# Deformable convolution and mixture-of-experts convolution on one core: sampling in one run per band, one shared PSUM bank, and another order of table work

## The chip, the cores and the metric

The kernel runs on one core of a Trainium2 chip. Its engines work side by side: TensorE (PE; its weight loads are listed as PEld), VectorE (DVE), ScalarE (ACT), GpSimd (POOL) and SyncE (SP). Each takes its instructions in the order in which the program wrote them. SP, POOL and ACT also issue transfers (DMA). The metric is device time in microseconds, lower is better. Everything is in 32-bit floats.

## The reference

The input `x` has 8 images of 128 channels and 64 x 64 pixels. Two layers follow each other, each `x + layer(groupnorm(x))` with 32 groups.

```python
# layer 0: modulated deformable convolution, 3x3, then batch norm and relu
om   = conv3x3(x, off_w) + off_b                 # 27 maps: 9 y shifts, 9 x shifts, 9 masks
py   = row + ky - 1 + off_y;  px = col + kx - 1 + off_x
val  = bilinear(x, py, px) * sigmoid(mask)       # zero outside the image
out  = einsum('bckhw,ock->bohw', val, w) + b
out  = relu(batchnorm(out) * gamma + beta)
...
# layer 1: four expert convolutions 3x3, mixed per image by a gate, plus a shared one
scores  = sigmoid(mean(x) @ gate_w.T + gate_b)
weights = top2(scores) / sum
out = einsum('ebchw,be->bchw', conv3x3(x, expert_w), weights) + conv3x3(x, shared_w) + biases
```

A branch for shifts larger than the kernel's reach exists (`general`); with these inputs the shifts are small and it isn't taken.

## The kernel before

**Dense stage (layer 0).** `dense` treats the bilinear sampling as a matrix product. An image is cut into 8 bands of 8 rows; over 8 images there are 64 bands, numbered `g`. For each band:

- `pick(g)` (DVE, L635) copies pixel windows into `picked`; `pixels(g)` (L643) transposes them on PE in four runs of 4, 4, 4 and 3 (`pt`, L650), and ACT copies each run to `xt` (L655).
- `load_x(g)` (2 transfers, L619) and `load_y(g, k)` (8 transfers, L603) bring tent weights from tables in device memory into `xwts` and `ywts`; POOL issues them two bands ahead.
- `weights(n)` (DVE, L677) multiplies them to `s`, for one of five groups of a band; it is called three groups ahead.
- `sample(n)` multiplies `xt` with `s` on PE: 12 instructions into a pair of PSUM banks (`pq`, L693). ACT copies the pair into `samples` (L703). For the first and the last group DVE also copies one column out of `pq` (L715, L717).
- `close(g)` (L719) copies edge rows, among them four rows that the next band's tile needs.
- `conv(g)` runs nine taps (`py`, L745; two instructions a tap) over `samples`; ACT adds the bias into `y` (L753), DVE takes statistics (L754), SP stores `y` (L755). An image's last band has two such runs, of 5 and 4 rows.

The order within a band is written out by hand (`manual_schedule`): the groups of band `g` come in chunks of 2, 2 and 1, and after each chunk a third of the taps of band `g - 1`, with transposes of band `g + 1` between them.

**The tables** of image `b + 1` are made while image `b` is worked on, by the generator `tables(b)`: each `next` on it emits work up to its next `yield`, and `pause(n)` skips `n` such steps. It loads the image (SP, L260), takes group statistics (DVE, L272), a small product for the group mean and one for the variance (`pm`, `pv`), normalises in place (L300, L301), forms the shift and mask maps `om` with four products (`combine` on DVE, L327, and `tap` on PE, L344), writes them to device memory by rows and by columns (`rowwise`, `colwise`) and reads them back (`raw_off`), turns them into distances and masks, then into five tents on ACT (`tent`, L462, L464), and stores them: 28 transfers for x (`store_x`, L506, all on SP) and one for y (`store_y`, L487). The generator is emptied at the start of band 6 of an image, and the next one begins there with the image load.

For the first image the chain runs alone, ahead of the first band (the head): early tents for the first rows on ACT, their stores on POOL and SP, then the loads of bands 0 and 1.

PSUM has eight banks. Before: `ps_c` two banks (products of the chain), `ps_q` two pairs, `ps_y` one, `ps_t` one.

**Layer 1** loads `y` and `x`, normalises, and runs 3x3 products with transformed rows (`vs`, four groups, L1245 to L1249) on PE (L1329). `prepare(b)` makes weights and rows of an image; `prepare(0)` runs to its end before the first product is written.

Of the kernel before, what the change touches and what calls it, by code (L numbers as in the profile page):

```python
# [56 lines left out]
EARLY = 2  # L57
OFF_AT = 16
# [7 lines left out]
def deform_moe_conv(  # L66
# [112 lines left out]
    def dense():  # L179

        with ExitStack() as st:
# [5 lines left out]
            ps_c = st.enter_context(tc.tile_pool(name="ps_c", bufs=2, space=PSUM))  # L187
            ps_q = st.enter_context(tc.tile_pool(name="ps_q", bufs=2, space=PSUM))
            ps_y = st.enter_context(tc.tile_pool(name="ps_y", bufs=1, space=PSUM))
            ps_t = st.enter_context(tc.tile_pool(name="ps_t", bufs=1, space=PSUM))  # L190
# [55 lines left out]
            xts, ss = {}, {}  # L246
            bands = [(b, j) for b in range(B) for j in range(NB)]

            def tables(b):

                def pause(n):
                    for _ in range(n):
                        yield
# [4 lines left out]
                for q in range(4):  # L258
                    rows = slice(16 * q, 16 * q + 16)
                    nc.sync.dma_start(  # L260
                        out=pad[:, ROWPAD + 16 * q : ROWPAD + 16 * q + 16],
                        in_=x[b].rearrange("c (h w) -> c h w", w=W)[:, rows],
                    )
                    yield from pause(5)
                yield from pause(3)
# [10 lines left out]
                yield from pause(6)  # L276
                pm = ps_c.tile([P, CH], F32, name="pm", tag="pc")
                nc.tensor.matmul(pm[:, 0:1], lhsT=gsel, rhs=mv[:, 0:1], start=True, stop=True)
                yield from pause(4)
# [6 lines left out]
                yield from pause(3)  # L286
                pv = ps_c.tile([P, CH], F32, name="pv", tag="pc")
                nc.tensor.matmul(pv[:, 0:1], lhsT=gsel, rhs=ev, start=True, stop=True)
                yield from pause(4)
# [5 lines left out]
                yield from pause(4)  # L295
# [60 lines left out]

                for j in (1, 2):
                    yield from combine(j)
                yield from pause(2)
                tap(1, 1)  # L360
                tap(1, 0)
                yield from pause(6)
                tap(1, 2)
                tap(2, 1)
                yield from pause(3)
                nc.scalar.activation(even, taken(1), AF.Identity, bias=offb_sb)
                yield from combine(0)
                yield
                tap(2, 0)
                tap(2, 2)  # L370
                yield from pause(3)
# [3 lines left out]
                yield  # L375
                yield from combine(3)
                tap(0, 1)
                tap(0, 0)
                yield from pause(6)
                tap(0, 2)  # L380
                tap(3, 1)
                yield from pause(3)
                nc.vector.tensor_tensor(even, even, taken(0), ALU.add)
                yield from pause(3)
                tap(3, 0)
                tap(3, 2)
                yield from pause(4)
# [10 lines left out]
                for j in range(4):  # L398
# [4 lines left out]
                    nc.gpsimd.dma_start(  # L403
# [14 lines left out]
                for k in range(3):  # L418
# [6 lines left out]
                    for outs, parts, v in places:  # L425
                        nc.sync.dma_start(out=raw_off[parts, v], in_=by_row[outs, 0::2, k])
                        parts = slice(W + parts.start, W + parts.stop)
                        nc.gpsimd.dma_start(
# [6 lines left out]
                yield from pause(24)  # L435
# [14 lines left out]
                for i in range(2):  # L450
                    nc.vector.tensor_scalar(
                        raw_off[:, 2 * i, 0], raw_off[:, 2 * i, 0], nudge[:, i : i + 1],
                        None, ALU.add,
                    )
                nc.vector.tensor_copy(by_x, moved(1, 0, "j", "u", "v"))
# [10 lines left out]
                if b == 0:  # L466
                    n = 2 * EARLY * XSTEP
                    for i in range(NR):
                        for _ in tent(early_x[:, i], dist[W:P, 0:n], i, sides[1]):
                            pass  # L470
                nc.vector.tensor_copy(by_y, moved(0, 0, "v", "j", "u"))
                nc.vector.tensor_copy(by_y[:, :, 0, 0], raw_off[sides[0], :, 0, 2 * W])
                nc.vector.tensor_copy(by_y[:, :, W - 1, 2], raw_off[sides[0], :, 0, W - 1])
                yield from pause(2)
# [11 lines left out]
                def store_y():  # L486
# [3 lines left out]
                            offset=y_table[b].offset + (NR - 1) * YSTEP,  # L490
                            ap=[[GROW, H], [GROW - YSTEP, NR], [1, YSTEP]],
# [923 lines left out]
```

## Time and profile before

| | us |
|---|---|
| runs shown | 1569.37, 1573.36, 1578.78 (median 1573.36) |
| the profiled execution, device time | 1568.24 |
| its span | 1566.5 |
| head, to the first sampling product | 90.6 |
| dense stage, to the last tap | 1182.6 |
| layer 1, to the end | 1566.5 |

| engine | busy us | share of the span |
|---|---|---|
| PE | 1406.3 | 90% |
| PEld | 773.4 | 49% |
| DVE | 882.8 | 56% |
| ACT | 704.5 | 45% |
| POOL | 544.4 | 35% |

The span runs from the first to the last instruction. A line of a timeline gives start, length, engine, source line, operation, output and inputs with shapes, and a count where equal neighbours are merged; the bracket at its end is the idle time before it and what ended it. Lengths of matmuls overlap, since they are pipelined. "SPq" is a transfer issued by SP.

### The profile page before, as it was taken

The page shows a single profiled execution, that of the slowest core. Times are in us where ns is not written, and L with a number is a line of the kernel's source. Part 1 is how long each engine was busy: PE and PEld are TensorE (multiplying, and loading weights), DVE is VectorE, ACT ScalarE, POOL GpSimd, SP SyncE. Part 2 cuts the span into 40 slices and gives each one's busy share as a digit, 9 for nine tenths or more (in the row PEclk, how much of TensorE's full clock was granted, in tenths as well). Part 3 has the DMA queues.
Part 4 walks back from the last instruction along what each step waited for, and adds up shares of the span by engine and source line. Part 5 has one row for each costly group of instructions (what it writes and reads, how often), then busy time and mean ns, then how long its engine had stood idle before and what let it go on. Part 6 is the DMA issues. An engine that isn't in the chain of part 4 may idle for free.

```text
span 1566.5 us, 21056 instructions
## 1 busy us (share of the span) xinstructions
PE 1406.3 (90%) x7714; PEld 773.4 (49%) x7714; DVE 882.8 (56%) x1764; ACT 704.5 (45%) x1000; POOL 544.4 (35%) x856
## 2 busy tenths in 40 slices
PE   4069979998998999899999989999993799999998
PEld 1045545655555555555555555556552344444443
DVE  6345545546544654655455365533326888898872
ACT  2334634654464456447446644654543332333320
POOL 3543432533442343335335333533303222222200
PEclk9579989999999999999999999999996899999999
DMA  6366685887488657848856794777817144444111
GB/s 200 91 130 140 155 198 131 158 196 165 107 176 184 148 126 175 210 102 182 197 141 136 173 218 101 179 164 187 189 55 271 54 161 154 155 161 161 41 55 56
DMA packets 156414, 234.33 MB, mean 150 GB/s; under 512 B 104362, under 2 KB 110958, under 8 KB 147982
## 3 DMA queue, kind: packets, MB, share of 16 engines
q0 software_dynamic: 62304, 124.77, 36.3%
q1 hardware_dynamic: 93116, 107.91, 23.3%
q8 instruction: 62, 1.02, 0.3%
q14 instruction: 50, 0.41, 0.1%
q10 hardware_dynamic: 882, 0.22, 0.1%
HBM read 180.23 MB, written 52.32 MB: 148 GB/s over the span
## 4 chain that ended last, share of the span: by engine, by line
PE 72%; DMA 11%; ACT 4%; DVE 4%; SPq 2%; issue 2%; POOL 1%; DVEq 0%; POOLq 0%; ACTq 0%
PE py L745 27%; PE pc L1329 20%; PE pq L693 14%; PE pt L650 5%; PE pc L344 5%; DMA pad<-in_x_dram 3%; DMA xwts<-tabx 2%; DMA ywts<-taby 2%; DMA tabx<-work 2%; ACT samples L703 1%; SPq L506 1%; ACT pad L300 1%; ACT y L753 1%; DMA yd<-y 1%; DMA xt<-in_x_dram 1%
## 5 line engine op out<-in xcount | busy, mean ns | idle before, releaser
L745 PE MATMUL py<-samples,dw_sb 128*128 128x512 f32 (+3 forms) x1296 | 601.6, 575 | 17.3 <-ACT y L753 17.3
L603 POOL DMA_DIRECT2D ywts<-taby x504 | 294.2, 603 | 460.3 <-DVE s L677 270.7
L703 ACT COPY samples<-pq 128x864 f32<-128x864 f32 (+1 forms) x320 | 295.5, 963 | 193.0 <-PE pq L693 193.0
L693 PE MATMUL pq<-s,xt 64*128 64x144 f32 (+1 forms) x3840 | 314.0, 306 | 46.5 <-DVE s L677 45.0
L693 PEld LDWEIGHTS pq<-s,xt 64*128 64x128 f32 x3840 | 261.4, 190 | 151.9 <-issue 90.0
L745 PEld LDWEIGHTS py<-samples,dw_sb 128*128 128x128 f32 x1296 | 214.6, 190 | 170.5 <-issue 122.2
L677 DVE TENSOR_TENSOR s<-xwts,ywts 128x432 f32<-128x432 f32 (+1 forms) x448 | 208.4, 496 | 101.0 <-PE pq L693 90.2
L655 ACT COPY xt<-pt 128x512 f32<-128x512 f32 (+1 forms) x256 | 143.2, 559 | 229.5 <-PE pt L650 225.5
L650 PEld LDWEIGHTS pt<-ident,picked 128*128 128x128 f32 x960 | 121.1, 141 | 136.4 <-issue 120.1
L1329 PE MATMUL pc<-v,u 128*128 128x512 f32 x384 | 172.8, 599 | 9.3 <-DVE u L1278 9.3
L1329 PE MATMUL pc<-v,wmix 128*128 128x512 f32 x384 | 176.5, 605 | 0.0
L650 PE MATMUL pt<-ident,picked 128*128 128x128 f32 x960 | 148.7, 275 | 8.6 <-ACT xt L655 4.6
L754 DVE BATCH_NORM_STATS2 ystats<-y 128x6 f32<-128x512 f32 (+3 forms) x72 | 45.6, 633 | 144.5 <-ACT y L753 144.5
L717 DVE COPY samples<-pq 128x24 f32<-128x24 f32 x64 | 12.9, 202 | 192.4 <-ACT samples L703 192.4
L1329 PEld LDWEIGHTS pc<-v,u 128*128 128x128 f32 x384 | 72.4, 190 | 98.3 <-issue 85.6
L1329 PEld LDWEIGHTS pc<-v,wmix 128*128 128x128 f32 x384 | 72.6, 192 | 89.0 <-issue 85.3
L619 POOL DMA_DIRECT2D xwts<-tabx x132 | 75.9, 582 | 109.0 <-DMA tabx<-work 57.1
L1307 ACT ACTIVATE t<-pc,bmix 128x512 f32<-128x512 f32 x32 | 22.0, 687 | 183.2 <-PE pc L1329 101.2
L753 ACT ACTIVATE y<-py,db_sb 128x512 f32<-128x512 f32 (+3 forms) x72 | 45.9, 638 | 97.5 <-PE py L745 93.6
L635 DVE COPY picked<-pad 128x960 f32<-128x960 f32 x128 | 83.4, 693 | 0.0
L327 DVE TENSOR_TENSOR combo<-pad 128x1024 f32<-128x1024 f32 x64 | 75.2, 1217 | 9.9 <-PE pc L344 9.4
L1157 POOL TENSOR_TENSOR x<-x,xt 128x512 f32<-128x512 f32 x32 | 46.5, 1483 | 86.0 <-ACT x L1155 86.0
(154 smaller groups left out, 1024.3 us busy)
## 6 DMA issues: line engine op xcount, KB each, us to landing
xwts<-tabx POOLq DMA_DIRECT2D x126, 576.0 KB, 9.5
ywts<-taby POOLq DMA_DIRECT2D x504, 90.0 KB, 5.7
pad<-in_x_dram SPq DMA_DIRECT2D x48, 512.0 KB
out_dram<-yo SPq DMA_DIRECT2D x32, 512.0 KB
yd<-y SPq DMA_DIRECT2D x48, 256.0 KB
pad<-yd SPq DMA_DIRECT2D x16, 512.0 KB
x<-yd SPq DMA_DIRECT2D x16, 512.0 KB
xt<-in_x_dram SPq DMA_DIRECT2D x16, 512.0 KB
```

The lines of the kernel that those rows point to most:

```text
L327: nc.vector.tensor_tensor(combo_of[j][:, half * n : half * n + n], *rows, op)
L344: nc.tensor.matmul(pcs[j][32 * q : 32 * q + 32].rearrange("p (h w) -> p h w", w=W)[:, :, lo:hi], lhsT=weight_of[j][:, kx], rhs=combo_of[j] ...
L603: engine.dma_start(out=y_wts[g % 2][at : at + NR * Q, r].rearrange("p a b c -> p (a b c)"), in_=bass.AP(tensor=y_table[b].tensor, offset=y ...
L619: engine.dma_start(out=x_wts[g % 3][HALF * h : HALF * h + HALF, slot * XSTEP : (slot + n) * XSTEP], in_=bass.AP(tensor=x_table[b].tensor, ...
L635: nc.vector.tensor_copy(picked[g % 2][:, :, h], bass.AP(tensor=one.tensor, offset=one.offset, ap=[list(one.ap[0]), [T, NCOL], [W, Q], [1, Q]],
L650: nc.tensor.transpose(pt[:, c], picked[g % 2][:, c0 + c].rearrange("p h y x -> p (h y x)"), ident,)
L655: nc.scalar.copy(xts[g][:, c0 : c0 + n], pt[:, 0:n])
L677: nc.vector.tensor_tensor(s[:, :, 3 * at : 3 * (at + k)].rearrange("p m (c x) -> p m c x", x=3), by_x[:, :, c : c + k], by_y[:, :, w : w + ...
L693: nc.tensor.matmul(by_m[:, h, :, at : at + k], lhsT=xts[g][rows, c], rhs=s[rows, :, at : at + k], start=True, stop=True,)
L703: nc.scalar.copy(bass.AP(tensor=one.tensor, offset=one.offset + first, ap=[list(one.ap[0]), [M * PLANE, 2], [PLANE, M], [WB + 1, 3], [1, w ...
L745: nc.tensor.matmul(py, lhsT=dw_sb[:, 3 * (2 - yy) + 2 - xx], rhs=samples[g % 2][:, m : m + 3 * n - 2 : 3, xx, 1 : W + 1], start=(i == 0), ...
L1329: nc.tensor.matmul(pc, lhsT=us[j][:, kx], rhs=vs[g][:, rows, kx : kx + W], start=(kx == 0), stop=(kx == 2),)
```

## The change

- PSUM: `ps_c` has one bank instead of two, and the transposes `pt` use it too; `ps_q` has three pairs instead of two; `ps_t` is gone.
- In a band all five groups are sampled first, then come all taps, with transposes after taps 0, 1, 5 and 6. The chain's PE work is marked by a `yield BLOCK` and goes only after taps 3 and 8, one block at a time, a block being all three taps of one product. Transposes' second `yield` is gone.
- The two column copies out of PSUM per band become two copies inside `samples`, in `close`. `close` and the statistics of `y` are put off (`late`) until after the second group of the next band.
- The image load leaves `tables` for a generator of its own (`load_image`), which starts in the middle of band 5 instead of at band 6. Pauses in `tables` are changed, most of them shortened.
- Of the x stores of an image, two thirds are issued by SP and one third by POOL.
- For the first image: `colwise` stores are split between POOL and SP, reads of `colwise` between POOL and ACT; early tents are made by DVE (three operations each) instead of ACT; y distances come before x distances; `store_y` goes tent by tent; `load_y(0)` is issued by SP and ACT in turn; the second image's chain stops at its first block until band 0 is done.
- In layer 1 `prepare(0)` is left once its weights are ready, and the row transforms of groups 1 to 3 are emitted between the first products.

```diff
-            ps_c = st.enter_context(tc.tile_pool(name="ps_c", bufs=2, space=PSUM))
-            ps_q = st.enter_context(tc.tile_pool(name="ps_q", bufs=2, space=PSUM))
+            ps_c = st.enter_context(tc.tile_pool(name="ps_c", bufs=1, space=PSUM))
+            ps_q = st.enter_context(tc.tile_pool(name="ps_q", bufs=3, space=PSUM))
             ps_y = st.enter_context(tc.tile_pool(name="ps_y", bufs=1, space=PSUM))
-            ps_t = st.enter_context(tc.tile_pool(name="ps_t", bufs=1, space=PSUM))
...
+            def load_image(b):
+                if b >= B:
+                    return
+                for q in range(4):
+                    rows = slice(16 * q, 16 * q + 16)
+                    nc.sync.dma_start(
+                        out=pads[b % 2][:, ROWPAD + 16 * q : ROWPAD + 16 * q + 16],
+                        in_=x[b].rearrange("c (h w) -> c h w", w=W)[:, rows],
+                    )
+                    yield from pause(4)
...
+                def block(j):
+                    yield BLOCK
+                    for kx in (1, 0, 2):
+                        tap(j, kx)
+                    yield from pause(2)
...
-                        store_x(i, 0, (nc.sync,))
-                        yield from pause(4)
-                    store_y()
+                        store_x(i, 0, (nc.sync, nc.sync, nc.gpsimd))
+                        yield from pause(2)
+                    store_y(0, NR)
...
-                    pt = ps_t.tile([P, 4, P], F32, name="pt")
+                    pt = ps_c.tile([P, 4, P], F32, name="pt", tag="pc")
...
-                by_h = t[:, 6:30].rearrange("p (h m) x w -> p h m x w", h=2)
-                if q == 0:
-                    nc.vector.tensor_copy(by_h[:, :, :, 2, 1], by_m[..., 0])
-                if q == NGR - 1:
-                    nc.vector.tensor_copy(by_h[:, :, :, 0, W], by_m[..., wide - 1])
...
+                nc.vector.tensor_copy(t[:, 6:30, 2, 1], t[:, 6:30, 0, 0])
+                nc.vector.tensor_copy(t[:, 6:30, 0, W], t[:, 6:30, 2, W + 1])
...
-                    nc.vector.bn_stats(ystats[:, b, j + e, :], y)
+                    late.append((nc.vector.bn_stats, ystats[:, b, j + e, :], y))
...
-            CHUNKS = (2, 2, 1)
+                for q in range(NGR):
+                    if g < len(bands):
+                        weights(g * NGR + q + AHEAD)
+                        sample(g * NGR + q)
+                        if q == 0:
+                            load_x(g + 2, nc.gpsimd)
+                        if q in (2, 3):
+                            for k in range(T * (q - 2), T * (q - 1)):
+                                load_y(g + 2, k, nc.gpsimd)
+                    if q == 1:
+                        put_off()
+                taps = conv(g - 1) if g else iter(())
+                twice = 2 if g and bands[g - 1][1] == NB - 1 else 1
+                for done, _ in enumerate(taps):
+                    part, odd = divmod(done, twice)
+                    if odd == 0 and part in PIXELS:
+                        next(turned, None)
+                    if odd == 0 and part in BLOCKS and asked:
+                        asked = False
+                        tick()
+                    for _ in range(3 + (g < NB) if twice == 1 else 1 + done % 2):
+                        tick()
+                    if odd == 0 and part == 4:
+                        if g + 2 < len(bands):
+                            pick(g + 2)
+                        if j == NB - 3:
+                            loads = load_image(b + 2)
...
+                made[b] = vs, (wmix[:, 0], u1, u2, wmix[:, 2]), bmix
                 for g in range(NG):
                     if b or g:
                         transform(g, 1, nc.vector)
...
-            for _ in prepare(0, made):
-                pass
+            first = prepare(0, made)
+            while 0 not in made:
+                next(first)
```

`tick` advances the image load and, if no block is waiting, the chain; `put_off` runs what `late` holds.

## The prediction

> **What bounds the kernel now.** I read the busy shares first (TensorE, PE, 90%; VectorE, DVE, 56%; ScalarE, ACT, 45%), then PE's row in tables of stretches. The dense stage, from the first full band to the last, is this row (length, then busy time of PE, PEld, DVE, ACT, POOL, granted clock, DMA share, GB/s):
>
> ```profile
> 100.00:1182.00 1082.00, 1033.94 (x6712) 603.73 (x6711) 534.53 (x1129) 558.84 (x766) 410.43 (x689) 0.98 0.70 158
> ```
>
> PE is idle for only 48 of 1082 us, so the order of PE's own work is what counts, and a quiet band (no table work in it) shows what it costs. The timeline of PE, one full band (start, length, instruction, count; I use start to start, since lengths overlap):
>
> ```profile
> 1114.68 1.87 PE L693 MATMUL pq<-s,xt 64*128 64x216 f32 x24
> 1116.48 1.14 PE L745 MATMUL py<-samples,dw_sb 128*128 128x512 f32 x2
> 1117.46 0.60 PE L650 MATMUL pt<-ident,picked 128*128 128x128 f32 x4
> 1117.90 1.92 PE L745 MATMUL py<-samples,dw_sb 128*128 128x512 f32 x4
> 1119.65 0.60 PE L650 MATMUL pt<-ident,picked 128*128 128x128 f32 x4
> 1120.18 1.74 PE L693 MATMUL pq<-s,xt 64*128 64x144 f32 x24
> 1121.85 2.02 PE L745 MATMUL py<-samples,dw_sb 128*128 128x512 f32 x4
> 1123.71 0.60 PE L650 MATMUL pt<-ident,picked 128*128 128x128 f32 x4
> ...
> 1125.12 1.13 PE L693 MATMUL pq<-s,xt 64*128 64x144 f32 x12
> 1126.18 1.15 PE L745 MATMUL py<-samples,dw_sb 128*128 128x512 f32 x2
> ...
> 1129.34 0.89 PE L693 MATMUL pq<-s,xt 64*128 64x216 f32 x8
> ```
>
> The band takes 1129.34 - 1114.68 = 14.66 us with no wait. Sampling (pq) comes in three runs of two, two and one groups: 1.80, 1.67 and 1.06 us. Let a run cost a fixed f, a plain group m, a wider end group e: f+e+m = 1.80, f+2m = 1.67, f+e = 1.06, so m = 0.74, f = 0.19, e = 0.87. A tap of the convolution (two py instructions) between two pt takes (1119.65 - 1117.90)/2 = 0.875; next to a pq run it is 0.98, and two such taps 1.86 instead of 1.75. Four pt take 0.44 before py, 0.53 before pq. So each border of a pq run costs its neighbour 0.1 as well.
>
> Who waits for whom, from PE's table of waits (total, times, longest):
>
> ```profile
> PE pq L693 <- DVE s L677: 45.0, 5, 21.5
> PE pm L278 <- DVE mv L275: 38.2, 4, 24.6
> PE py L745 <- ACT y L753: 17.3, 15, 1.5
> ```
>
> The two longest belong to the head (before the first band). The other 23.5 and 13.6 us lie where one image ends and the next begins. There the timelines of SP, POOL and DVE read:
>
> ```profile
> 615.91 5.94 SPq L260 DMA_DIRECT2D pad<-in_x_dram  x4
> 616.12 1.11 POOL L619 DMA_DIRECT2D xwts<-tabx  x2 [10.76 <-DMA tabx<-work]
> 630.35 1.29 DVE L272 BATCH_NORM_STATS2 stats<-pad 128x6 f32<-128x512 f32 x2 [6.65 <-DMA pad<-in_x_dram]
> ```
>
> The image load starts only when the table stores in front of it on SP are out; POOL's table loads wait for the same stores; all then move at once (DMA share 1.04 from 620 to 640 us), and DVE, which runs in order, stands at the statistics while PE wants `s`.
>
> **The change, part by part.** Sums are against the profiled execution: span 1566.5, device time 1568.2 us. The three runs shown have median 1573.4, so I add 5.1 at the end.
>
> *Sampling in one run.* Two of three runs fall away in each of the 63 bands that have both sampling and taps: per run f = 0.19 plus two borders of 0.1, so 0.78 us a band, 49 us. That holds if the copies out of PSUM keep up:
>
> ```profile
> 1115.91 1.85 ACT L703 COPY samples<-pq 128x1008 f32<-128x1008 f32 x2 [0.38 <-PE pq L693]
> 1121.24 1.72 ACT L703 COPY samples<-pq 128x864 f32<-128x864 f32 x2 [0.36 <-PE pq L693]
> ```
>
> Clocking the new band from the start of its run: the groups end at 0.19+0.87 = 1.06, 1.80, 2.54, 3.28, 4.15. The first copy starts at 1.23 (1115.91 - 1114.68), the next 0.93, 0.80, 0.80, 0.80 later (a pair spans 1.85 or 1.72 where its last copy alone has 0.92): 1.23, 2.16, 2.96, 3.76, 4.56, ending at 2.26, 3.08, 3.88, 4.68, 5.59. With three pairs the fourth group needs the first copy (2.26, wanted 2.54), the fifth the second (3.08, wanted 3.28). Both fit, by 0.2 us. With two pairs the third group would wait for 2.26 instead of 1.80, and three hand-overs would give back nearly all of 0.78.
>
> The Trainium skill ("TensorEngine Tiling (Array Packing)", PSUM Bottleneck) speaks against this part: row tiling speeds up TensorE but not the emptying of PSUM, so the copy can become the limit. The row does show ACT (4.36 us for five) slower than PE (4.15); were the taps to wait for the last copy (5.59), the band would take 15.3 us and the part would lose 41 us instead of gaining 49; but the taps read the band before, so PE needs only the three pairs.
>
> *One PSUM bank for pt, pc, pm, pv.* A second pt run needs the copy of the first. Tap 0 ends at 5.13, pt 5.57, its copy runs 5.7 to 6.3 behind the last sample copy; tap 1 ends at 6.44. It fits by 0.1. The later pair (after taps 5 and 6) has the same spacing without copies ahead. Table products come in four runs of 24 in place of six of 16 (L344, 1.84 us for 16, 0.106 each at a steady pace, so about 0.15 a run and 0.2 of borders): two fewer for 7 images, 3 to 5 us, I take 3. In the head the four products lose their overlap with the readers of the bank: about 1.8 us.
>
> *Column fix and `close`.* 128 small DVE copies (L715 and L717, 0.20 us) out of PSUM become 128 inside SBUF. No row shows the new form; bounds 0.15 (the smallest DVE copies) and 0.28 (L725, 192 elements). Nothing on DVE here is on the path: what counts is that `close` now stands behind `s` of the fifth group (free to start at 1.2), bn_stats (0.69) and the fixes: 1.2+0.75+0.6+0.2+0.54 = 3.3 us into the band; the taps want it at 4.15. Cover 0.85 us. In bands with table work (combine, 1.2 us each, picked 1.28) DVE can come in 2 us late; then first the taps wait, then `s`.
>
> *Waits of py for y.* Of 17.3 us, about half are waits of 1.10 in bands where tents sit in front of y on ACT (seven); they are covered by the 4.15 us of sampling now: -8. The rest, between the two parts of an image's last band, stays. But the same tents now push the first sample copy: y at 1.95 in place of 0.8 moves PE's fourth group by 0.6. With the late `close`: +8 in all (bounds 0 and 40: no band, or 5 of 8 bands of 7 images by 1.1 us).
>
> *Image loads and table stores.* Loads are issued from the middle of the sixth band, some 10 us sooner; x stores go 2:1 to SP and POOL (SP L506 takes about 0.83 us per issue, 28 an image; POOL 0.6) and the pauses after the products shrink from about 96 to 75 steps, so the table is done more than a band before its load. What waits behind a POOL store for ACT's tent is the next table load, with some 4 us to spare. At stake: 37 us, and 9 for the slow matmuls after each stall (12 pq in 1.81 instead of 1.01 us at 496.9, clock 0.85). The bytes remain: the image's 2.1 MB and about 2.9 MB for the bands (1.2 MB of xwts and 0.7 of ywts a band, y out) in 18 us is above the 254 GB/s seen there, so I leave 2 to 3 us at each of six places: -30 (bounds -10 and -46).
>
> The skill ("DMA: Bandwidth & Descriptors", on issuing engines not being separate queues) says a second issuing engine saves only sequencer time. By that alone the two-queue part would be worth nothing once bytes bind, as the share of 1.04 says they do; the start 10 us earlier is what my number rests on.
>
> *Head.* First pq is at 90.59 because DVE stood for 19.4 us at shift L297 (POOL's pow behind table loads). That is now after the first band. But band 1 (103.07 now) needs `ywts` of its own, the last of POOL's loads (issued till 88.05, 5.7 to land). POOL's chain is 0.7 later by my count (products +1.8, split colwise and raw loads -1.9 and -0.8, by_y before by_x +1.1, early tents 15 DVE operations of about 0.25, bounds 0.15 and 0.41, for 10 on ACT of 3.4 in all): 94.5, then three `s`, picks, pm and pv, 4.5 us: 99. So -4 (bounds -10 and +2).
>
> *Layer 1 head.* DVE is busy without a gap from 1204 to 1236.9 and PE waits 9.5 us for its mv. The transforms are reordered, none removed: 0 (bounds -4 and +2).
>
> Sum: -49 -3 -8 +8 -30 -4 = -86: 1482 profiled, 1487 as a median.
>
> **The rivals.**
> (a) Copies or the shared bank set the pace: the 0.1 to 0.2 us of room is not there, and the 0.78 is given back. For: the room is small. Against: the clocking above. 1573 - 37 = 1536.
> (b) The change at the image border does not do what it says: bytes bind, and the stall only moves: -49-3-4-8+8+0 = -56: 1517.
> (c) Slower: `close` late on DVE. If DVE comes to it more than 0.85 us late, every tap row waits. It costs more than all gains together when PE waits 86/63 = 1.4 us in each band, that is DVE 2.2 us late in each. If all bands with table work (5 of 8, 39) waited 3 us: +117-86: 1604. For: DVE holds statistics and combines in order. Against: DVE is busy 534 of 1082 us, and quiet bands leave it idle for half their length.
>
> **How the numbers follow.** Forecast 0.64, (a) 0.16, (b) 0.13, (c) 0.07. The time is the forecast's 1487. Low end: border and head at their better bounds (-16 and -6), 1465; high end 1538, to take in (b) and (a). A difference under 0.5% (8 us) can't be told from none. Faster 0.91, same 0.02, slower 0.07.
>
> **What would show it.** After: a quiet band of 13.9 us with one pq run of 60 and about 4.2 us; hardly any wait of pq or pm for DVE in the dense stage; first pq near 76 and band 1 near 99 us; layer 1 as long as before. Wrong if pq waits for ACT's copies, pt for xt, or py for `close` in most bands.

## The result and the profile after

The changed kernel takes 1586.93 us (median of 7 runs, 1582.18 to 1589.91); the kernel before, run beside it on the same chip, takes 1577.12 us (7 runs). The ratio is 1.0064, 95% interval 1.0039 to 1.0089: 0.6% slower, where 5.5% faster was forecast. All ratios below are to the kernel before on the same chip. Line numbers differ from kernel to kernel (the sampling product is L693 before and L690 after); the tile names are the same. The profiled execution has device time 1584.7 and span 1582.8 us (before: 1568.2 and 1566.5).

The same row of the dense stage as before, from the first full band to the last (length, busy time of PE, PEld, DVE, ACT, POOL, granted clock, DMA share, GB/s):

```profile
100.00:1199.00 1099.00, 988.14 (x6652) 594.94 (x6648) 534.37 (x1128) 547.22 (x764) 441.92 (x743) 0.96 0.70 156
```

PE is idle for 111 us here; before it was 48. So PE's own work became shorter by 46 us (a few of these because 60 instructions had already run before 100 us), and its waits longer by 63. The timeline of PE in a quiet band shows the first half of this:

```profile
1119.01 4.25 PE L690 MATMUL pq<-s,xt 64*128 64x216 f32 x60
1123.19 1.15 PE L739 MATMUL py<-samples,dw_sb 128*128 128x512 f32 x2
1124.18 0.60 PE L648 MATMUL pt<-ident,picked 128*128 128x128 f32 x4
1124.62 1.04 PE L739 MATMUL py<-samples,dw_sb 128*128 128x512 f32 x2
...
1131.17 1.92 PE L739 MATMUL py<-samples,dw_sb 128*128 128x512 f32 x4
1133.02 4.25 PE L690 MATMUL pq<-s,xt 64*128 64x216 f32 x60
```

One run of 60 sampling instructions, no wait in it, and 14.01 us from run to run where it was 14.66. PE's table of waits over the whole execution shows the second half:

```profile
PE pq L690 <- DVE s L674: 84.7, 13, 25.5
PE pt L648 <- ACT xt L653: 30.8, 8, 17.4
PE pm L283 <- DVE mv L280: 23.0, 2, 12.4
...
PE pq L690 <- ACT samples L700: 11.0, 7, 1.7
```

The wait of 25.5 is the one before the first band. Of the other 59 us of `pq` for `s`, 53 lie at the borders of images 1 to 5 (in the kernel before, `pq` waited 45.0 for `s`, 21.5 of it before the first band); at the border of image 0 PE waits 12.4 us for `mv`. A border is the stretch around bands 6 and 7 of an image, where the image after next is loaded. One of these, in the timelines of PE, SP, POOL and DVE in turn:

```profile
622.16 4.21 PE L690 MATMUL pq<-s,xt 64*128 64x216 f32 x60
636.06 2.60 PE L690 MATMUL pq<-s,xt 64*128 64x216 f32 x36
651.77 3.49 PE L690 MATMUL pq<-s,xt 64*128 64x144 f32 x24 [13.10 <-DVE s L674]
```

```profile
625.38 1.02 SPq L259 DMA_DIRECT2D pad<-in_x_dram  x1
626.85 3.13 SPq L504 DMA_DIRECT2D tabx<-work  x4
630.36 0.63 SPq L485 DMA_DIRECT2D taby<-work  x1
631.04 2.59 SPq L259 DMA_DIRECT2D pad<-in_x_dram  x2
633.74 0.99 SPq L749 DMA_DIRECT2D yd<-y  x1
634.78 0.49 SPq L259 DMA_DIRECT2D pad<-in_x_dram  x1
```

```profile
632.07 1.15 POOL L617 DMA_DIRECT2D xwts<-tabx  x2 [7.33 <-DMA tabx<-work]
```

```profile
639.11 1.29 DVE L277 BATCH_NORM_STATS2 stats<-pad 128x6 f32<-128x512 f32 x2 [6.62 <-DMA pad<-in_x_dram]
645.86 1.29 DVE L277 BATCH_NORM_STATS2 stats<-pad 128x6 f32<-128x512 f32 x2 [5.46 <-DMA pad<-in_x_dram]
649.83 1.29 DVE L277 BATCH_NORM_STATS2 stats<-pad 128x6 f32<-128x512 f32 x2 [2.68 <-DMA pad<-in_x_dram]
651.03 1.25 DVE L674 TENSOR_TENSOR s<-xwts,ywts 128x432 f32<-128x432 f32 x3
```

The same border in the kernel before, PE and SP:

```profile
610.83 1.87 PE L693 MATMUL pq<-s,xt 64*128 64x216 f32 x24
635.33 1.81 PE L693 MATMUL pq<-s,xt 64*128 64x144 f32 x12 [3.35 <-DVE s L677]
```

```profile
614.55 0.65 SPq L487 DMA_DIRECT2D taby<-work  x1
```

Band 6 of image 3 starts at 622.16 (before: 610.83). The first image quarter is issued 3.2 us later, the other three 9 to 13 us later, behind x stores in SP's order; before, all four went out 5 to 11 us after that band's start. The y table's store stands 8.2 us behind the band's start; before it was 3.7. DVE takes all eight statistics ahead of the `s` that band 7 needs for its fourth group, and waits for each quarter; before, three stood ahead of the `s` that PE waited for, and the other five behind it.

How the time is spread over the images (to the last `y` of each, from the timeline of ACT, in us), with the forecast's terms added up per image (0.78 a band, 0.4 for products, 5 a border, 4 for the head):

| image | before | after | difference | forecast |
|---|---|---|---|---|
| 0, with the head | 252.5 | 268.9 | +16.4 | -15 |
| 1 | 134.0 | 129.3 | -4.7 | -12 |
| 2 to 5, mean of the four | 138.3 | 141.6 | +3.3 | -12 |
| 6, no new image to load | 129.7 | 127.3 | -2.4 | -7 |
| 7, no tables to make | 113.2 | 107.3 | -5.9 | -6 |
| layer 1 | 383.9 | 383.6 | -0.3 | 0 |

Image 7, with sampling and taps alone, is as forecast, in part by luck: 2.2 of its 5.9 us are one wait of PE in the kernel before (`pn` for `near`, 1085.25 in its trace) that the forecast didn't count. Image 6, which makes tables and loads no image, is off by 4 us, images 1 to 5, which do both, by 7 to 15. The table products don't fall into the same images in both kernels: images 0, 1 and 6 hold 240, 48 and 96 of their instructions (`pc`) where it was 224, 80 and 80, at 0.11 us each, so that 3.5 of image 1's 4.7 us only moved to other images.

### The profile page after: what moved, and what is told of

Same layout as the page of the kernel before. It is cut to its first block, busy times and chain, and to the rows that moved or that the text cites. A ratio compares the mean times of both kernels' runs of the same rounds, so it can differ in the third digit from the quotient of the medians.

```text
span 1582.8 us, 21300 instructions
## 1 busy us (share of the span) xinstructions
PE 1365.4 (86%) x7714; PEld 769.1 (49%) x7714; DVE 884.0 (56%) x1779; ACT 691.1 (44%) x990; POOL 573.6 (36%) x909
## 4 chain that ended last, share of the span: by engine, by line
PE 72%; DMA 12%; DVE 5%; ACT 4%; issue 3%; SPq 3%; POOL 1%; ACTq 0%; DVEq 0%; POOLq 0%
PE py L739 27%; PE pc L1345 20%; PE pq L690 13%; PE pt L648 6%; DMA pad<-in_x_dram 5%; PE pc L349 5%; DMA xwts<-tabx 3%; DMA tabx<-work 1%; SPq L504 1%; DMA ywts<-taby 1%; ACT samples L700 1%; ACT y L747 1%; DMA taby<-work 1%; DMA colwise<-om 1%; DVE combo L332 1%
## 5 line engine op out<-in xcount | busy, mean ns | idle before, releaser
L739 PE MATMUL py<-samples,dw_sb 128*128 128x512 f32 (+3 forms) x1296 | 573.6, 561 | 7.9 <-ACT y L747 6.1
L690 PE MATMUL pq<-s,xt 64*128 64x144 f32 (+1 forms) x3840 | 291.5, 306 | 95.7 <-DVE s L674 84.7
L700 ACT COPY samples<-pq 128x864 f32<-128x864 f32 (+1 forms) x320 | 282.6, 975 | 145.4 <-PE pq L690 145.4
L690 PEld LDWEIGHTS pq<-s,xt 64*128 64x128 f32 x3840 | 264.0, 194 | 141.5 <-issue 93.5
L674 DVE TENSOR_TENSOR s<-xwts,ywts 128x432 f32<-128x432 f32 (+1 forms) x448 | 198.5, 497 | 204.9 <-PE pq L690 116.6
L739 PEld LDWEIGHTS py<-samples,dw_sb 128*128 128x128 f32 x1296 | 219.1, 190 | 157.5 <-issue 126.8
L648 PEld LDWEIGHTS pt<-ident,picked 128*128 128x128 f32 x960 | 112.0, 142 | 175.4 <-ACT xt L653 108.0
L648 PE MATMUL pt<-ident,picked 128*128 128x128 f32 x960 | 153.3, 280 | 35.0 <-ACT xt L653 30.8
L617 POOL DMA_DIRECT2D xwts<-tabx x132 | 79.5, 613 | 65.9 <-DMA tabx<-work 41.5
L277 DVE BATCH_NORM_STATS2 stats<-pad 128x6 f32<-128x512 f32 x64 | 40.8, 683 | 88.3 <-DMA pad<-in_x_dram 88.3
L1172 POOL TENSOR_TENSOR pad<-pad,pad 128x512 f32<-128x512 f32 x28 | 39.5, 1442 | 71.7 <-ACT pad L1170 71.5
```

What stands on the lines that cost most here:

```text
L617: engine.dma_start(out=x_wts[g % 3][HALF * h : HALF * h + HALF, slot * XSTEP : (slot + n) * XSTEP], in_=bass.AP(tensor=x_table[b].tensor, ...
L648: nc.tensor.transpose(pt[:, c], picked[g % 2][:, c0 + c].rearrange("p h y x -> p (h y x)"), ident,)
L674: nc.vector.tensor_tensor(s[:, :, 3 * at : 3 * (at + k)].rearrange("p m (c x) -> p m c x", x=3), by_x[:, :, c : c + k], by_y[:, :, w : w + ...
L690: nc.tensor.matmul(by_m[:, h, :, at : at + k], lhsT=xts[g][rows, c], rhs=s[rows, :, at : at + k], start=True, stop=True,)
L700: nc.scalar.copy(bass.AP(tensor=one.tensor, offset=one.offset + first, ap=[list(one.ap[0]), [M * PLANE, 2], [PLANE, M], [WB + 1, 3], [1, w ...
L739: nc.tensor.matmul(py, lhsT=dw_sb[:, 3 * (2 - yy) + 2 - xx], rhs=samples[g % 2][:, m : m + 3 * n - 2 : 3, xx, 1 : W + 1], start=(i == 0), ...
```

## The experiments

**Is the gain of the run real, and what carries it?** Three kernels with two pairs of `pq`. The first (e1) is the kernel before with one edit:

```diff
-            CHUNKS = (2, 2, 1)
+            CHUNKS = (5,)
```

> The kernel before, with its five sample groups in one run and the taps behind them; two pairs of pq, the column fixes and the table chain stay as they were. Theory (the run itself is what gains, 0.65 us a band in quiet bands): with two pairs the third and later groups of a run wait some 0.1 us each for an ACT copy of 0.86 us against 0.84 us of products, so 0.3 to 0.65 us of 63 bands come back: -20 to -40 us, ratio 0.975 to 0.987. Rival (the third pair makes the gain): PE waits for ACT a full copy at each of three groups, 0.9 us or more a band against 0.65 saved: ratio 1.00 or above, and a wait of pq for samples above 50 us in all.

Measured: 1633.12 us, ratio 1.0374 (1.0330 to 1.0418). PE's waits in it:

```profile
PE pq L693 <- DVE samples L715: 51.7, 55, 2.0
PE pq L693 <- DVE s L677: 41.1, 6, 21.9
...
PE pq L693 <- ACT samples L703: 30.1, 51, 8.9
```

A quiet band takes 15.5 us. The theory missed: the run alone loses. The pair is held first by DVE's column copy out of PSUM, which waits for ACT's copy of the same samples, then by ACT's. The next kernel (e5) separates the two; it is the changed kernel with

```diff
-            ps_c = st.enter_context(tc.tile_pool(name="ps_c", bufs=1, space=PSUM))
-            ps_q = st.enter_context(tc.tile_pool(name="ps_q", bufs=3, space=PSUM))
+            ps_c = st.enter_context(tc.tile_pool(name="ps_c", bufs=2, space=PSUM))
+            ps_q = st.enter_context(tc.tile_pool(name="ps_q", bufs=2, space=PSUM))
```

> The changed kernel with two pairs for pq and two banks for the products and the transposes, in place of three and one; the run of five groups and the column fix in SBUF stay. e1_run_alone lost 0.85 us a band, and its waits name the column copies of each pair (samples, 51.7 us) before the ACT copies (30.1 us). Theory A (the column copies out of PSUM held the pairs): with the fix in SBUF two pairs cost only what ACT's copy is longer than the group and its notice, 0.1 to 0.5 us a band: +6 to +30 us against the changed kernel. Theory B (two pairs are too few in any case): as in e1, 1.0 to 1.5 us a band: +60 to +95 us. The second bank may give back 1 to 2 us at each image (waits of pc and pm for xt).

Measured: 1628.83 us, ratio 1.0342 (1.0313 to 1.0371), 44 us above the changed kernel: between the two theories. In a quiet band, which takes 15.2 us, the run of 60 is cut in three (timeline of PE):

```profile
1182.36 1.87 PE L690 MATMUL pq<-s,xt 64*128 64x216 f32 x24
1184.68 1.81 PE L690 MATMUL pq<-s,xt 64*128 64x144 f32 x24 [0.45 <-ACT samples L700]
1186.75 1.13 PE L690 MATMUL pq<-s,xt 64*128 64x144 f32 x12 [0.27 <-ACT samples L700]
1187.81 1.15 PE L739 MATMUL py<-samples,dw_sb 128*128 128x512 f32 x2
```

From 1182.36 to 1187.81 it is 5.45 us in place of 4.18. The two waits, 0.45 and 0.27, make 0.72 of the 1.27; the rest fits the run's fixed cost (0.19 by the forecast), paid again at each cut with some loss of overlap, which no run measured apart. So the third pair is what turns the run from a loss into a gain, and the column fix in SBUF is worth the 0.3 us a band between e1 and this.

The third (e11) puts the column fix into e1 (the copies out of PSUM go, two come into `close`), and so differs from e5 by the chain, the borders and the head:

```diff
-                if q == 0:
-                    nc.vector.tensor_copy(by_h[:, :, :, 2, 1], by_m[..., 0])
-                if q == NGR - 1:
-                    nc.vector.tensor_copy(by_h[:, :, :, 0, W], by_m[..., wide - 1])
...
+                nc.vector.tensor_copy(t[:, 6:30, 2, 1], t[:, 6:30, 0, 0])
+                nc.vector.tensor_copy(t[:, 6:30, 0, W], t[:, 6:30, 2, W + 1])
```

> The kernel before with the run of five groups and the column fix in SBUF, but two pairs, and its own table chain, image loads and head: against e5_two_pairs it differs by the chain, the borders and the head alone, against e1_run_alone by the column fix alone. Theory (chain, borders and head of the change cost some 25 to 40 us net where -37 was forecast): the quiet band is 15.1 us as in e5, and the time is that much below e5: ratio to before 1.008 to 1.02. Rival (chain and head cost nothing net, and the run's gain is smaller than the quiet bands say): as e5, 1.03 to 1.04.

Measured: 1626.05 us, ratio 1.0301 (1.0269 to 1.0333), quiet band 15.2 us. Against e5 the old chain and head save some 6 us only, hardly more than the noise, not 25 to 40. At the borders the old chain is no better here than the new one in e5: from the y of band 5 to the y of band 6 it takes, in images 0 to 5, 26.8, 23.6, 24.5, 25.6, 22.3 and 26.1 us, in all 148.9 (e5: 149.2), against 129.3 before and 165.5 in the changed kernel. Of the 20 us more than before the slower quiet band (0.5 us a band) explains 3.

It is tempting to put the other 17 to the single run itself. e1 stands against that: it has the same run and the same chain, and takes 131.4 us there in all. DVE's order doesn't explain it either: in e11, as before and in e1, three statistics stand ahead of the `s` that PE waits for. At the border of image 3 the first of them waits for its quarter until 666.54 in e11, 15.1 us after the quarter's issue, and until 664.03 in e1, 10.6 us after it. Why the quarter lands later in one of two kernels that differ in the column fix alone stays open.

**The head.** The changed kernel (e2) with image 1's chain driven two steps further before band 1:

```diff
-                    for _ in range(4):
+                    for _ in range(6):
                         next(made)
```

> The changed kernel with image 1's table chain driven two steps further before band 1, so that the pow of its scale stands on POOL ahead of the table loads of band 3. Theory (pow behind POOL's table loads holds shift, the normalisation on ACT behind it, the copies xt and so the transposes): the wait of 17.4 us of pt in band 1's taps goes to under 4, and the time falls by 12 to 17 us: ratio to before 0.995 to 0.999. Rival (band 1 to 3 wait for the x tables or the image's bytes in any case): the stall turns up at pq (for s, behind xwts) in band 2 or 3, and the time moves by less than 4 us.

First the changed kernel's own head, in the timelines of PE and POOL:

```profile
94.01 6.33 PE L690 MATMUL pq<-s,xt 64*128 64x216 f32 x58
...
124.89 0.90 PE L648 MATMUL pt<-ident,picked 128*128 128x128 f32 x3 [17.36 <-ACT xt L653]
```

```profile
109.22 1.13 POOL L617 DMA_DIRECT2D xwts<-tabx  x2
110.38 3.36 POOL L601 DMA_DIRECT2D ywts<-taby  x6
117.19 0.56 POOL L601 DMA_DIRECT2D ywts<-taby  x1 [3.44 <-DMA xwts<-tabx]
120.07 0.56 POOL L601 DMA_DIRECT2D ywts<-taby  x1 [2.32 <-DMA xwts<-tabx]
120.64 0.57 POOL L299 TENSOR_TENSOR scale<-ve,nhalf 128x1 f32<-128x1 f32 x1
```

Band 1 starts sampling at 94.01, earlier than the 103 us of before, and then its taps stop for 17.36 us. The 0.57 us of `pow` wait behind the table loads of two bands. `shift` on DVE waits for it, the normalisation on ACT for `shift` (17.56 us idle at L305), the copy `xt` stands behind that on ACT, and PE wants `xt`. In the edited kernel the same two lines are

```profile
106.91 0.57 POOL L299 TENSOR_TENSOR scale<-ve,nhalf 128x1 f32<-128x1 f32 x1
```

```profile
114.80 0.90 PE L648 MATMUL pt<-ident,picked 128*128 128x128 f32 x3 [6.89 <-ACT xt L653]
```

and image 0 ends at 260.8 in place of 268.9. Time: 1580.51 us, ratio 1.0042 (1.0015 to 1.0070). In the trace 8 us come back, half of what was expected: `shift` now stands on DVE behind four `s`, which wait 11.3 us for band 2's x table (to 109.46). The times alone can't tell this from the changed kernel.

**The borders.** The changed kernel (e3) with each quarter loaded when its rows are free (`load_image` here takes the quarters to load as a second argument):

```diff
-                        if j == NB - 3:
-                            loads = load_image(b + 2)
+                        freed = {0: 0, 2: 1, NB - 4: 2, NB - 3: 3}
+                        if g < len(bands) and j in freed:
+                            loads = load_image(b + 2, (freed[j],))
```

> The changed kernel with each quarter of the image after next loaded as soon as the last band that reads its rows has been picked (in bands 0, 2, 4 and 5) in place of all four in band 5 to 6. Theory (the stall of 12 to 13 us of pq at each image border comes from statistics waiting for quarters that land late, ahead of s in DVE's order): three of four quarters are there long before, only the last is waited for, and at each of six borders 7 to 11 us go: -40 to -65 us against the changed kernel, ratio to before 0.965 to 0.98. Rival (the border is bound by the bytes of the x table's stores and the table loads, the image counts little): the wait of statistics goes but s then waits for xwts as long; less than 15 us go, ratio 0.997 or above.

Measured: 1560.33 us, ratio 0.9907 (0.9876 to 0.9939). (Here the first quarter of image 2, one of 24, isn't loaded, since band 0 of image 0 has no taps in which the step falls.) 25 us less than the changed kernel, below the range expected. The wait tables from 270 to 1070 us say where the rest went. PE's waits for `s` fall from 58.6 to 5.6 us, but its waits for `y` rise from 4.1 to 17.8 and those for `mv` from nothing to 16.0. DVE, changed kernel:

```profile
DVE stats L277 <- DMA pad<-in_x_dram: 71.5, 18, 6.9
DVE shift L302 <- POOL scale L299: 14.7, 5, 4.5
DVE s L674 <- DMA xwts<-tabx: 1.5, 2, 0.8
```

and the kernel with spread quarters:

```profile
DVE s L674 <- DMA xwts<-tabx: 40.5, 7, 8.2
DVE shift L302 <- POOL scale L299: 32.7, 5, 8.6
```

The statistics wait no more, and two other waits take their place: `s` for the x table's loads, which wait for the x stores, and `shift` for a `pow` behind POOL's loads, as in the head.

Next, the gate of the chain's products (e4):

```diff
-            PIXELS, BLOCKS = (0, 1, 5, 6), (3, 8)
+            PIXELS, BLOCKS = (0, 1, 5, 6), range(9)
```

> The changed kernel with the 24 table products and the two small ones let in at any of the nine taps, not only at the fourth and ninth; the chain then ends some 40 steps (a band and a half) sooner. Theory (the gate makes the chain late: x stores end some 8 us after the border band's start, and the image's loads stand behind them on SP): the stores end before that band, the image's quarters are issued some 5 to 10 us sooner, and 4 to 8 us go at each of six borders: -25 to -45 us against the changed kernel, less 3 us for more changes of product shape. Rival (the quarter's landing is set by bytes, or statistics stand ahead of s in any case, and an earlier chain changes nothing): within 8 us of the changed kernel.

Measured: 1564.73 us, ratio 0.9932 (0.9903 to 0.9961): 21 us less than the changed kernel. At the border of image 3 the x stores now end 20 us before band 6 starts (596.9 against 617.4), and the statistics hardly wait for the image (2.3 us from 270 to 1070 us). PE waits 30.6 us for `s` there in place of 58.6. What holds DVE instead is the y table's loads:

```profile
DVE s L674 <- DMA ywts<-taby: 91.8, 11, 13.0
```

Is it the place behind the x stores on SP that makes the image late? The changed kernel with the quarters on ACT's queue (e10):

```diff
-                    nc.sync.dma_start(
+                    (nc.scalar if b > 1 else nc.sync).dma_start(
                         out=pads[b % 2][:, ROWPAD + 16 * q : ROWPAD + 16 * q + 16],
```

> The changed kernel with the image's four quarters issued on ACT's queue in place of SP's, at the same steps. Theory (the quarters are late because they stand behind the x stores on SP): they go out some 5 to 8 us sooner and PE's wait at a border falls by as much, -20 to -40 us against the changed kernel. Rival (the DMA engines are near 1.0 in that stretch, and the x stores, the table loads and the quarters share the bytes): the quarters start sooner and land hardly sooner, or the x table does later: less than 10 us of gain.

Measured: 1585.67 us, ratio 1.0050 (1.0030 to 1.0070): nothing. At the border looked at above, DVE, POOL and PE now read:

```profile
635.46 1.29 DVE L277 BATCH_NORM_STATS2 stats<-pad 128x6 f32<-128x512 f32 x2 [0.93 <-DMA pad<-in_x_dram]
639.81 0.76 DVE L674 TENSOR_TENSOR s<-xwts,ywts 128x432 f32<-128x432 f32 x2 [2.56 <-PE pq L690]
652.88 1.79 DVE L674 TENSOR_TENSOR s<-xwts,ywts 128x432 f32<-128x432 f32 x4 [10.86 <-DMA xwts<-tabx]
```

```profile
636.33 1.14 POOL L617 DMA_DIRECT2D xwts<-tabx  x2 [10.21 <-DMA tabx<-work]
```

```profile
655.09 0.56 PE L283 MATMUL pm<-mv,gsel 128*128 128x1 f32 x2 [7.60 <-DVE mv L280]
```

The last statistics end at 636.8 instead of 651, and PE gains little: the next band's x table arrives at 652.9, the `s` that waited for it hold `mv` behind them on DVE, and PE stands at `pm`. From 270 to 1070 us PE waits 12.0 us for `s` (58.6 in the changed kernel), but 27.0 for `mv` and 13.2 for `y` (nothing and 4.1). Two paths end close to each other, quarters to statistics to `s`, and x stores to x loads to `s`; taking one away shows the other. With both paths touched at once, products at any tap and the quarters on ACT's queue (e12):

```diff
-            PIXELS, BLOCKS = (0, 1, 5, 6), (3, 8)
+            PIXELS, BLOCKS = (0, 1, 5, 6), range(9)
...
-                    nc.sync.dma_start(
+                    (nc.scalar if b > 1 else nc.sync).dma_start(
```

> e4 (products let in at any tap) with the image's quarters on ACT's queue: the quarters keep their time in the border stretch and no longer stand behind the x stores on SP. e6 differs from it only in that three of the quarters are loaded bands earlier. If the order on SP is what e6 took away beyond e4 (25 us), this gives it too: ratio to before 0.975 to 0.983. If it is the bytes of the image in the stretch in which x stores and table loads move as well (in e4 the statistics hardly waited for the image, but s waited for ywts), this is as e4, 0.990 to 0.997.

Measured: 1556.33 us, ratio 0.9883 (0.9855 to 0.9911), between its two theories: some 8 us beyond e4, little more than the noise of the two. With products at any tap and the quarters spread as in e3, now in bands 1, 3, 4 and 5 (e6):

```diff
-            PIXELS, BLOCKS = (0, 1, 5, 6), (3, 8)
+            PIXELS, BLOCKS = (0, 1, 5, 6), range(9)
...
+                        freed = {1: 0, 3: 1, NB - 4: 2, NB - 3: 3}
+                        if g < len(bands) and j in freed:
+                            loads = load_image(b + 2, (freed[j],))
```

> The changed kernel with both edits of the image borders: the 24 products let in at any tap, and the image's quarters loaded in bands 1, 3, 4 and 5. Theory (two separate delays at a border, the late quarter and the late x stores): the gains of e3 and e4 add up in good part, -35 to -50 us against the changed kernel, ratio to before 0.973 to 0.985. Rival (what remains at a border is bound by bytes, with the DMA engines near 1.0 of their time from the x stores to the first loads of the new tables): no more than the better of the two alone, ratio 0.988 to 0.994.

Measured: 1540.73 us, ratio 0.9776 (0.9746 to 0.9805): 45 us below the changed kernel, the gains of e3 and e4 added up. e6 differs from e12 in that three quarters of an image, 1.6 MB, move out of the border stretch, the last goes out some 6 us sooner (counted from the start of band 6), and all four are back on SP; that is worth 17 us (11 between the two traces). In e12 the statistics hardly waited for the image any more (7.9 us from 270 to 1070), so the quarters' own landing can't be worth that much. It speaks for the bytes: when they move counts for more than SP's order.

Two more shifts of the chain lost. Statistics 18 steps later, on top of e4 (e7):

```diff
-                yield from pause(12)
+                yield from pause(30)
```

> e4 (products let in at any tap) with the statistics 18 steps later in the chain, so that most of them stand behind the s of the border's second band on DVE. Theory (statistics ahead of s hold PE at the border): the waits of pq for s fall from 57 us to under 35 and the time by 8 to 20 us against e4, ratio to before 0.98 to 0.988. Rival (in e4 the quarters have landed when the statistics come, and s waits for the y table's loads): within 5 us of e4, or slower since the chain ends later.

Measured: 1576.30 us, ratio 0.9985 (0.9964 to 1.0006), 8 us worse than e4. The waits of `pq` for `s` fell as expected (57.2 to 32.5 us), but `pt` for `xt` rose from 29.3 to 44.3 and `pm` for `mv` from 18.0 to 33.8. And the chain of e6 without its first twelve steps of pause, with the edit of the head (e8; the parts of e6 aren't shown again):

```diff
-                yield from pause(12)
                 stats = small.tile([P, NCH, 6], F32, name="stats")
...
-                    for _ in range(4):
+                    for _ in range(6):
                         next(made)
```

> The edits of e6 and e2 together, and the chain without its first twelve steps of pause, since three quarters have long landed when it starts: pow then comes on POOL ahead of the table loads of the border's second band. Theory (pow behind the table loads is the delay that e3 uncovered at the border, as in the head): against e6 5 us less at the head and 2 to 5 us at each of six borders, ratio to before 0.96 to 0.975. Rival (the last quarter is waited for again since the statistics come sooner, or bytes bind): no better than e6.

Measured: 1568.20 us, ratio 0.9948 (0.9930 to 0.9967), 27 us worse than e6. Its largest wait of DVE for a transfer:

```profile
DVE combo L444 <- DMA combo<-colwise: 96.4, 8, 17.8
```

Here DVE comes to the offsets before they are back from device memory, and the `s` behind them in its order wait too. An earlier chain isn't better in itself; each step has to come after its data.

**The version that beats both.** e6 with the head's edit, the first pause left at 12 (e9; the parts of e6 aren't shown again):

```diff
-                    for _ in range(4):
+                    for _ in range(6):
                         next(made)
```

> The three edits that helped, together: quarters loaded as their rows come free, products at any tap, and image 1's pow ahead of band 3's table loads; the chain keeps its first pause. Theory (the head's wait is separate from the borders): 5 to 9 us less than e6, ratio to before 0.970 to 0.975, better than both kernels. Rival (the wait moves to the next band's x table in the head, as the earlier chain of e8 moved to a wait for the gathered offsets): within 4 us of e6, ratio 0.975 to 0.980.

Measured: 1526.73 us (6 runs, 1520.91 to 1543.46), ratio 0.9705 (0.9656 to 0.9754): 3% faster than before, 3.6% faster than the change. Image 0 ends at 259.4 us, images 2 to 5 take 131.3 on average (before: 138.3).

## Why the prediction was wrong

**"Sampling in one run", -49: right, and nearly the size.** 0.65 us for a quiet band against 0.78, or 41 us over 63 bands. The clocking of the copies, with 0.2 us of room at the fourth and fifth group, held: `pq` waited for copies 11.0 us in all. It also gave what two pairs would do ("nearly all of 0.78" given back); e5 shows it was mild, two pairs lose 0.5 us more than that. Rivals (a) and (c) fall: taps waited for `close` once, 1.8 us.

**"Table products", -3: too small to be seen.** Image 6, which has products and no image to load, gained 2.4 us of the 7. Most of what is missing isn't the products' cost: PE waits there 1.05 us for `s` (986.82 in the trace) and 1.74 for a sample copy (1008.35), each in a band with two products, and a run of 16 product instructions (1.84 us) falls into image 6 that fell into image 5 before.

**"Waits of py for y", -8, and late copies and `close`, +8: right.** `py` waits 6.1 us for `y` where it was 17.3; `pq` waits 11.0 for sample copies where it was 1.5, and `py` 1.8 for `close`.

**"Image loads and table stores", -30: this step failed; the six borders lost time.** From the y of band 5 to that of band 6 they took 165.5 us in all in place of 129.3. The step rested on three statements. "Loads are issued ... some 10 us sooner": the generator begins sooner, but on SP its transfers stand behind x stores that wait for ACT's tents, and the last three quarters are later against the band than before. "...the table is done more than a band before its load": I counted pauses (96 to 75 steps) and left out the waits at six gates, each open only after taps 3 and 8; the table is 8 us behind the band's start, and e4, which opens the gates, gets 21 us back. And I had said that DVE "stands at the statistics while PE wants `s`", and didn't ask where the statistics stand in the new order: with the first pause at 12 steps all eight stand ahead of band 7's `s`. What share the single run has in the loss stays open, since e11 lost 17 us here under the old chain and e1 didn't.

Rival (b) had a good part of the mechanism, that bytes bind and the stall only moves, and too kind a price: it put 0 for the borders. e10 shows the stall moving, and e6 against e12 speaks for the bytes; the late chain, which e4 shows, isn't in it. The Trainium skill ("DMA: Bandwidth & Descriptors", on issuing engines not being separate queues), which I had weighed and set aside, says that a second issuing engine saves only sequencer time. e10 agrees in its time (ratio 1.0050 against 1.0064), though the last statistics ended 14 us sooner; in e12, with the stores out of the way, the same move was worth some 8 us.

**"Head", -4: this step failed too.** The part that I clocked was right or too careful: first `pq` at 75.4 (forecast 76), band 1 at 94.0 (99). But I wrote that POOL's `pow` "is now after the first band" and costed the move at nothing. It had moved behind four more sets of POOL's loads, and its readers, `shift`, the normalisation and with it `xt`, are in the way of band 1's taps: 17.4 us. e2 shows the mechanism, and gets 8 of the 17 us back.

**"Layer 1 head", 0: right** (383.9 and 383.6 us).

By image the forecast missed 31 us in image 0, 7 in image 1, 15 in each of images 2 to 5 and 4 in image 6, together 102: the whole difference. The edits of e9 get 57 of it back (1.0064 to 0.9705 of 1577). Against the forecast, e9 still has 22 us too many in image 0, 12 in image 1 and 5 in each of images 2 to 5, and 5 too few in image 6. What the remaining 45 consist of stays open; no run had the borders without any wait, and the forecast's 2 to 3 us left at each may never have been to be had.

Of the signs that the prediction named for being wrong (`pq` waiting for copies, `pt` for `xt`, `py` for `close` in most bands) none came: they watched the regrouping, and the loss lay in the loads and in POOL's order. It shows in the sign of being right that failed, "hardly any wait of pq or pm for DVE": `pq` waits 53 us for `s` at the borders.

## What to carry to other kernels

When a step moves, list every queue that it now stands in and what stands ahead of it there: a `pow` of 0.57 us behind table loads, and four image quarters behind stores, cost more than the regrouping of 3840 products won. Where two paths end at the same wait, an experiment that shortens one can show nothing; shorten both, and first spread the bytes over the time in which the DMA engines are less busy (their share is 0.22 to 0.81 from 560 to 600 us in the changed kernel, and 1.01 to 1.05 from 636 to 652).

## What the runs showed of the hardware

After PE's stall of 13.1 us at the border, the next 24 sampling products took 3.49 us where they take 1.87 otherwise, at a granted clock of 0.60 from 652 to 656 us and 1.00 from 656 on:

```profile
652.00:656.00 4.00, 4.00 (x26) 3.11 (x27) 3.77 (x11) 1.61 (x2) 3.43 (x6) 0.60 0.97 217
656.00:660.00 4.00, 4.00 (x18) 2.12 (x17) 0.00 (x0) 1.50 (x3) 1.12 (x3) 1.00 0.99 158
```

So this stall cost 1.6 us more than its own length. A shorter one can cost the same: in e1 the 24 products after a wait of 3.06 us took 3.49 us as well (668.30 in its trace), and after one of 1.86 us 2.16 (812.02). The clock of 0.85 that the prediction put beside the slow products at 496.9 is that of 620 to 640 us; from 494 to 500 it was 0.50.

Cutting a run of 64-row products was dearer than the wait that cut it: in e5 two waits of 0.72 us together made the run 1.27 us longer.
